# A four-layer graph network on one core: the setup moved into the static plan, six shared PSUM banks, and a plan with other durations

## The chip, the cores and the metric

The kernel runs on one core of one Trainium2 chip. The metric is device time in microseconds (us) of that core, from the first to the last instruction. Five engines work side by side, each through its own queue in program order: TensorE (PE, with its weight loads PEld), VectorE (DVE), ScalarE (ACT), GpSimd (POOL) and SyncE (SP), which here issues nearly all DMA transfers.

## What is computed

64 graphs of 256 nodes with 256 features pass four layers, each with a layer norm before it and a residual after it. Layers 0 and 1 are attention with four heads of 64, layer 2 attention with one head of 256, layer 3 a gated graph network of three rounds.

```python
h = relu(layernorm(x)); x = x + gat0(h, adj)      # 4 heads: softmax over neighbours, elu
h = relu(layernorm(x)); x = x + gat1(h, adj)      # 4 heads, relu + residual, norm per head
h = relu(layernorm(x)); x = x + gat2(h, adj)      # 1 head of 256
h = relu(layernorm(x))
for i in range(3):                                # layer 3
    m = h @ weight[i]
    aggr = A.T @ m                                # A = (adj != 0)
    h = gru_cell(aggr, h, w_ih, w_hh, b_ih, b_hh)
x = x + h
```

`adj` is 0 or 1 (about 1.6% ones), all numbers are fp32.

## The kernel before

The graphs are worked on in 32 pairs. The program is a list of steps, each with its engine, an assumed duration, the steps it needs, and the buffers that it takes and gives back. When the kernel is built, a list scheduler (the plan) goes through these steps, always takes the one that can start first (by rank among those that can start at the same time), and writes its instructions. On the chip each engine runs its instructions in that order and waits on semaphores; the assumed durations act only through the order.

```python
class Plan:
    AFTER = {"PE": 0.25, "DVE": 0.12, "ACT": 0.22, "POOL": 0.2, "SP": 0.1}   # handoff after a step
    ...
    def run(self):
        ...
                t = max(t, clock[s[0]])          # s[0]: the engine
                starts.setdefault(s[0], []).append((t, k))
```

Before the plan stands the setup. It loads the weights, adds columns to them that give the attention scores (multiply by the attention vectors and reduce), and multiplies the GRU's input weights by the layer weights, so that a GRU round needs one product less:

```python
    nc.sync.dma_start(w0e[:, :, :D], w0.rearrange("(c p) f -> p c f", p=P))
    ...                                                   # w1e, w2e, whh, rows of bias, gamma, beta
    with tc.tile_pool(name="setup", bufs=1) as sp, tc.tile_pool(name="setup_ps", bufs=2, space=PSUM) as spp:
        ...                                               # loads of vectors (ACT queue), w3, wih
        for i in range(L):
            for dc in range(DC):
                for g0, g1 in ((0, 512), (512, G)):
                    ps = spp.tile([P, 512], F32, name="ps_wc")
                    for ec in range(DC):
                        nc.tensor.matmul(ps[:, : g1 - g0], lhsT=w3[:, i, ec, dc * P : (dc + 1) * P],
                                         rhs=wih[:, ec, g0:g1], start=(ec == 0), stop=(ec == DC - 1))
                    nc.scalar.copy(wc[:, i, dc, g0:g1], ps[:, : g1 - g0])
```

PSUM is shared out by purpose: `w` (two tiles of two banks: projection and head sums), `t` (one bank, all transposes of the attention part), `g` (three banks, the GRU).

```python
    TILES = {
        "w": tiles("w", 2, [2, S], pool=psum), "t": tiles("t", 1, [S], pool=psum), "g": tiles("g", 3, [S], pool=psum),
        "xt": tiles("xt", 4, [C, D]), "at": tiles("at", 2, [C, N], I32), ...
        "ht3": tiles("ht3", 3, [DC, S]), "hn": tiles("hn", 3, [C, D]), ..., "d": tiles("d", 2, [S]), ...
```

One attention layer of one graph: project, copy the scores out (`scores`, VectorE), transpose them, send them through DRAM so that each partition gets the whole row (`a_b`), then per head exponential (ACT), mask (DVE) and sum (TensorE, 65 columns, the last one gives the denominator):

```python
        k = add("PE", 1.8, emit_project, [g.done], take=[pw, g.wh], give=[g.ht], due=due)
        g.scored = sc = add("DVE", 0.15, emit_scores, [k], due=due)
        wh = add("ACT", 0.57, emit_wh, [k, sc], give=[pw], due=due)
        k = add("PE", 0.12, emit_turn, [sc], take=[turn, er, g.dj], due=due)
        k = add("ACT", 0.45, emit_er, [k], give=[turn], due=due)
        k = add("SP", 0.1, emit_out, [k], give=[er], due=due, lag=2.0)
        load_ = add("SP", 0.1, emit_in, [k], take=[a_b], due=due, lag=3.0)
        k = None
        for h in range(heads):
            x_ = add("ACT", 0.94, lambda h=h: emit_exp(h), [load_, s.has_cap], take=[q[h]], ...)
            x_ = add("DVE", 0.84, lambda h=h: emit_q(h), [x_], ...)
            k = add("PE", 1.8 if heads == 1 else 1.0, lambda h=h: emit_sum(h), [x_, wh, k],
                    take=[] if h else [g.po], give=[q[h]], due=due)
        g.done = add("DVE", 0.17, emit_rs, [k], take=[g.rs], due=due)
```

The layer norm before each layer has its inverse root on GpSimd (`add("POOL", 1.0, emit_root, ...)`) between two VectorE steps. Of the GRU, only this matters here: its difference step writes a buffer `d`, and a pair's GRU is due three periods of 112 us after its attention, so that GRU matmuls of older pairs fill TensorE while younger pairs are in attention.

Of the kernel before, what the change touches and what calls it, by code (L numbers as in the profile page):

```python
# [32 lines left out]
class Plan:  # L33
# [7 lines left out]
    AFTER = {"PE": 0.25, "DVE": 0.12, "ACT": 0.22, "POOL": 0.2, "SP": 0.1}  # L41
# [11 lines left out]
    def run(self):  # L53
# [16 lines left out]
        while ready:  # L70
            best = None
            starts = {}
            for k, t in ready.items():
                s = steps[k]
                for b in s[4]:
                    t = max(t, min(self.free[b.tag])[0]) if self.free[b.tag] else None
                    if t is None:
                        break
                if t is None:
                    continue  # L80
                t = max(t, clock[s[0]])
                starts.setdefault(s[0], []).append((t, k))
# [32 lines left out]
def fast_path(ctx, tc, x, adj, w0, a0_src, a0_dst, w1, a1_src, a1_dst, bias1, gamma1, beta1,  # L115
# [8 lines left out]
    nc = tc.nc  # L124
# [22 lines left out]
    whh = consts.tile([P, DC, G], F32, name="whh")  # L147
    bg = consts.tile([P, 8], F32, name="bg")
# [6 lines left out]

    nc.sync.dma_start(w0e[:, :, :D], w0.rearrange("(c p) f -> p c f", p=P))
    for dc in range(DC):
        nc.sync.dma_start(
            w1e[:, dc, :D].rearrange("p (h e) -> p h e", h=H),
            w1[:, dc * P : (dc + 1) * P, :].rearrange("h p e -> p h e"),  # L160
        )
    nc.sync.dma_start(w2e[:, :, :D], w2t.rearrange("(c p) f -> p c f", p=P))
    nc.sync.dma_start(whh, whh_t.rearrange("(c p) g -> p c g", p=P))
    nc.sync.dma_start(bias_b, _rows(bias1, D))
    nc.sync.dma_start(gamma_b, _rows(gamma1, D))
    nc.sync.dma_start(beta_b, _rows(beta1, D))

    with tc.tile_pool(name="setup", bufs=1) as sp, tc.tile_pool(
        name="setup_ps", bufs=2, space=bass.MemoryType.PSUM
    ) as spp:  # L170
        ab = sp.tile([P, 3, 2, D], F32, name="ab")
        for s, (s0, s1) in enumerate(((a0_src, a1_src), (a0_dst, a1_dst))):
            nc.scalar.dma_start(ab[:, 0, s, :], _rows(s0, D))
            first = bass.AP(tensor=s1.tensor, offset=s1.offset, ap=[[0, P], [T * E, H], [1, E]])
            nc.scalar.dma_start(ab[:, 1, s, :].rearrange("p (h e) -> p h e", h=H), first)
        nc.scalar.dma_start(ab[:, 2].rearrange("p s f -> p (s f)"), _rows(a2, 2 * D))
        w3 = sp.tile([P, L, DC, D], F32, name="w3")
        wih = sp.tile([P, DC, G], F32, name="wih")
        for i in range(L):
            nc.sync.dma_start(w3[:, i], w3t[i].rearrange("(c p) d -> p c d", p=P))  # L180
        nc.sync.dma_start(wih, wih_t.rearrange("(c p) g -> p c g", p=P))
        bi = sp.tile([P, 6], F32, name="bi")
        bh = sp.tile([P, 6], F32, name="bh")
        nc.scalar.dma_start(bi, bih)
        nc.scalar.dma_start(bh, bhh)

        for k, (we, heads) in enumerate(((w0e, H), (w1e, H), (w2e, 1))):
            for dc in range(DC):
                for s in range(2):
                    tmp = sp.tile([P, D], F32, name="tmp", bufs=2)  # L190
                    nc.vector.tensor_mul(tmp, we[:, dc, :D], ab[:, k, s, :])
                    nc.vector.tensor_reduce(
                        we[:, dc, D + s * heads : D + (s + 1) * heads],
                        tmp.rearrange("p (h e) -> p h e", h=heads), AX.X, OP.add,
                    )


        for i in range(L):
            for dc in range(DC):
                for g0, g1 in ((0, 512), (512, G)):  # L200
                    ps = spp.tile([P, 512], F32, name="ps_wc")
                    for ec in range(DC):
                        nc.tensor.matmul(
                            ps[:, : g1 - g0],
                            lhsT=w3[:, i, ec, dc * P : (dc + 1) * P],
                            rhs=wih[:, ec, g0:g1],
                            start=(ec == 0),
                            stop=(ec == DC - 1),
                        )
                    nc.scalar.copy(wc[:, i, dc, g0:g1], ps[:, : g1 - g0])  # L210


        nc.vector.tensor_add(bg[:, 0:4], bi[:, 0:4], bh[:, 0:4])
        nc.vector.tensor_copy(bg[:, 4:6], bh[:, 4:6])
        nc.vector.tensor_scalar_mul(bg[:, 0:6], bg[:, 0:6], 0.5)
        nc.vector.tensor_copy(bg[:, 6:8], bi[:, 4:6])
# [13 lines left out]
    def tiles(tag, count, shape, dtype=F32, pool=bufs):  # L230
# [3 lines left out]
        "w": tiles("w", 2, [2, S], pool=psum),  # L234
        "t": tiles("t", 1, [S], pool=psum),
        "g": tiles("g", 3, [S], pool=psum),
        "xt": tiles("xt", 4, [C, D]),
        "at": tiles("at", 2, [C, N], I32),
# [12 lines left out]
        "ht3": tiles("ht3", 3, [DC, S]),  # L251
        "hn": tiles("hn", 3, [C, D]),
# [4 lines left out]
        "d": tiles("d", 2, [S]),  # L257
# [18 lines left out]

    PERIOD = 112.0
# [5 lines left out]
    def load(p, needs):  # L283
# [10 lines left out]
        s.has_x = add("SP", 0.1, emit_x, needs, take=[s.xt, s.scores], due=s.due, lag=5.0)  # L294
        s.has_a = add("SP", 0.1, emit_a, needs, take=[s.at], due=s.due, lag=5.0)
        return s

    def prepare(s):
# [42 lines left out]
        for b, ps in enumerate((Buf("t"), Buf("t"))):  # L341
            k = add(
                "PE", 0.46, lambda b=b, ps=ps: emit_turn(b, ps), [first, *caps, k],
# [8 lines left out]
    def norm(s, b, needs, sink):  # L352
# [3 lines left out]
        mv, rs, xn, ps = Buf("mv"), Buf("rstd"), Buf("xn"), Buf("t")  # L356
# [36 lines left out]
        k = add("POOL", 1.0, emit_root, [k], take=[rs], due=due)  # L393
        k = add("DVE", 0.82, emit_xn, [k], take=[xn], give=[rs, mv], due=due)
        t = add("PE", 0.46, emit_turn, [k], take=[ps] if sink else [ps, g.ht], give=[] if sink else [xn], due=due)
# [5 lines left out]
    def attend(s, b, g, layer, we, heads, alpha, score0):  # L401
# [4 lines left out]
        pw, turn, er, a_b = Buf("w"), Buf("t"), Buf("er"), Buf("a_b")  # L406
        g.wh = Buf("wh1" if heads == 1 else "wh4")
        g.po, g.dj, g.rs = Buf("w"), Buf("dj"), Buf("rs")
# [5 lines left out]
        def sums_():  # L414
            return g.po.t[:, :, : heads * (e + 1)].rearrange("p c (h e) -> p c h e", h=heads)
# [53 lines left out]
        def emit_sum(h):  # L469
            for ic in range(2):  # L470
                for jc in range(2):
                    nc.tensor.matmul(  # L472
                        g.po.t[:, ic, h * (e + 1) : (h + 1) * (e + 1)],
                        lhsT=q[h].t[:, jc, ic * P : (ic + 1) * P], rhs=g.wh.t[:, jc, h, :],
                        start=(jc == 0), stop=(jc == 1),
                    )

        def emit_rs():
            nc.vector.reciprocal(g.rs.t[:, :, :heads], sums_()[:, :, :, e])

        k = add("PE", 1.8, emit_project, [g.done], take=[pw, g.wh], give=[g.ht], due=due)
# [4 lines left out]
        k = add("SP", 0.1, emit_out, [k], give=[er], due=due, lag=2.0)  # L486
# [162 lines left out]
    def gru_layer(s, i, ht, hn, has_ht, has_hn):  # L649
# [32 lines left out]
        for dc in range(DC):  # L682
# [6 lines left out]
            )  # L689
            has_ag = has_ag + [k]  # L690

        users, has_new = [], []

        def column(j):
            nh, ri, ni, zi = Buf("g"), Buf("g"), Buf("g"), Buf("g")
# [642 lines left out]
```

## Time and profile before

| | |
|---|---|
| time, median of 3 runs | 3726.41 us (3721.69 to 3729.0) |
| profiled span | 3726.5 us, mean granted TensorE clock 0.982 |
| TensorE busy | 3567.1 us, 14577 matmul instructions |
| gate matmuls (128x512) | 4608, 603 and 596 ns each |
| head sums (128x65) | 4096, 278 ns each, paced 0.112 us apart |
| first transpose of a pair | 48.55 us after the start |
| first GRU aggregation | 186.11 us after the start |

Matmuls overlap in the pipeline, so their mean durations are longer than the pace at which they follow each other. Line numbers (L436) are those of the kernel printed above; an entry such as "PE t L436 <- DVE scores L428: 52.1, 16, 3.8" says who waited for whom, how long in all, how often, and the longest. In a timeline line the first two numbers are start and duration in us, and the bracket at its end tells how long the engine had been idle and who released it.

### The profile page before, as it was taken

How to read it: one execution, taken by the hardware profiler on the slowest of the kernel's cores; microseconds unless marked ns; L12 is line 12 of the kernel's file. 1: busy time of each engine (PE TensorE's matmuls, PEld its weight loads, DVE VectorE, ACT ScalarE, POOL GpSimd, SP SyncE). 2: the span in 40 equal slices, each digit the busy share in tenths (PEclk: the TensorE clock that was granted, in tenths of full speed). 3: DMA queues.
4: the chain of work that ended last, by engine and by line, in shares of the span. 5: the costliest groups of instructions: out<-in, count | busy, mean ns of one | idle time of the engine just before them, and what ended most of it. 6: DMA issues, size and time to landing. Idle time of an engine off the chain costs nothing.

```text
span 3726.5 us, 41332 instructions
## 1 busy us (share of the span) xinstructions
PE 3567.1 (96%) x14577; PEld 2258.2 (61%) x14577; DVE 2245.9 (60%) x5282; ACT 1594.5 (43%) x3277; POOL 1011.6 (27%) x1040
## 2 busy tenths in 40 slices
PE   5799999999999999999999999999999999999998
PEld 4565566666565666566666665666666665666654
DVE  4656665665566666565665566666566665665622
ACT  3343444444444444444444444444444444444422
POOL 1322322232222322322232222322223332222211
PEclk8799999999999999999999999999999999999999
DMA  3100101111100011101101111011001111010000
GB/s 115 43 29 29 43 21 43 38 31 52 32 32 32 29 49 32 32 32 43 38 29 45 30 41 33 26 52 32 32 32 43 35 31 43 21 45 30 21 6 12
DMA packets 86023, 133.49 MB, mean 36 GB/s; under 512 B 8368, under 2 KB 68784, under 8 KB 85808
## 3 DMA queue, kind: packets, MB, share of 16 engines
q1 hardware_dynamic: 84032, 129.98, 10.8%
q8 instruction: 117, 1.92, 0.2%
q10 hardware_dynamic: 1776, 0.79, 0.1%
q14 instruction: 98, 0.80, 0.1%
HBM read 113.38 MB, written 17.37 MB: 35 GB/s over the span
## 4 chain that ended last, share of the span: by engine, by line
PE 85%; DVE 7%; POOL 4%; DMA 1%; issue 1%; ACT 1%; SPq 0%; DVEq 0%; ACTq 0%; POOLq 0%
PE g L675 48%; PE w L472 15%; PE g L660 9%; PE w L422 8%; PE t L380 2%; PE g L762 2%; POOL rstd L367 2%; DVE xn L371 1%; PE t L323 1%; DVE xt L530 1%; POOL xm L521 1%; POOL xm L553 1%; DVE st L362 1%; POOL rstd L366 1%; PE t L436 1%
## 5 line engine op out<-in xcount | busy, mean ns | idle before, releaser
L675 PE MATMUL g<-ht,whh 128*128 128x512 f32 x2304 | 1106.8, 603 | 4.5 <-ACT n L699 4.4
L675 PE MATMUL g<-ag,wc 128*128 128x512 f32 x2304 | 1080.3, 596 | 0.0
L675 PEld LDWEIGHTS g<-ag,wc 128*128 128x128 f32 x2304 | 433.5, 192 | 508.5 <-issue 499.6
L716 POOL TENSOR_TENSOR d<-ht,n 128x512 f32<-128x512 f32 x192 | 284.4, 1481 | 1504.5 <-ACT n L713 1504.4
L472 PEld LDWEIGHTS w<-wh,q 128*128 128x128 f32 x4608 | 593.8, 196 | 87.8 <-issue 49.3
L675 PEld LDWEIGHTS g<-ht,whh 128*128 128x128 f32 x2304 | 416.1, 192 | 378.3 <-issue 359.1
L472 PE MATMUL w<-wh,q 128*128 128x65 f32 (+1 forms) x4608 | 619.5, 289 | 17.0 <-DVE q L463 14.1
L463 DVE SCALAR_TENSOR_TENSOR q<-q,dj,cap_t 128x256 f32<-128x256 f32 x1152 | 522.4, 512 | 101.5 <-ACT q L456 97.7
L456 ACT ACTIVATE q<-a_b,scores 128x256 f32<-128x256 f32 x1152 | 499.1, 498 | 136.8 <-DMA a_b<-dr 84.2
L719 DVE SCALAR_TENSOR_TENSOR d<-z,d 128x512 f32<-128x512 f32 x192 | 148.1, 772 | 379.6 <-ACT z L704 358.7
L660 PE MATMUL g<-am,hn 128*128 128x256 f32 x1536 | 363.4, 381 | 0.3 <-ACT z L704 0.3
L660 PEld LDWEIGHTS g<-am,hn 128*128 128x128 f32 x1536 | 286.0, 191 | 74.1 <-issue 34.2
L371 DVE TENSOR_SCALAR xn<-xt,mv,rstd 128x256 f32<-128x256 f32 x512 | 209.9, 431 | 162.2 <-POOL rstd L367 158.3
L704 ACT ACTIVATE r<-g,bg 128x512 f32<-128x512 f32 x192 | 131.6, 686 | 386.7 <-PE g L675 386.7
L707 DVE SCALAR_TENSOR_TENSOR n<-r,n 128x512 f32<-128x512 f32 x192 | 131.8, 686 | 265.2 <-ACT r L704 239.2
L713 ACT ACTIVATE n<-n,bg 128x512 f32<-128x512 f32 x192 | 137.8, 718 | 247.8 <-DVE n L710 247.6
L704 ACT ACTIVATE z<-g,bg 128x512 f32<-128x512 f32 x192 | 131.3, 684 | 258.0 <-PE g L675 253.6
L387 ACT ACTIVATE ht<-t 128x512 f32<-128x512 f32 x256 | 152.0, 594 | 188.7 <-PE t L380 170.3
L699 ACT ACTIVATE n<-g,bg 128x512 f32<-128x512 f32 x192 | 131.9, 687 | 233.6 <-PE g L675 230.4
L380 PEld LDWEIGHTS t<-ident,xn 128*128 128x128 f32 x1024 | 125.8, 145 | 143.2 <-issue 60.3
L362 DVE BATCH_NORM_STATS2 st<-xt 128x6 f32<-128x256 f32 x512 | 192.9, 410 | 26.4 <-DMA xt<-in_x_dram 25.9
L380 PE MATMUL t<-ident,xn 128*128 128x128 f32 x1024 | 170.8, 282 | 30.0 <-DVE xn L371 11.0
(86 smaller groups left out, 3536.2 us busy)
## 6 DMA issues: line engine op xcount, KB each, us to landing
a_b<-dr SPq DMA_DIRECT2D x128, 512.0 KB
xt<-in_x_dram SPq DMA_DIRECT2D x32, 512.0 KB
at<-in_adj_dram SPq DMA_DIRECT2D x32, 512.0 KB
out_dram<-hn SPq DMA_DIRECT2D x32, 512.0 KB
a_b<-dr SPq DMA_DIRECT2D x64, 128.0 KB
dr<-er SPq DMA_DIRECT2D x128, 4.0 KB
dr<-er SPq DMA_DIRECT2D x64, 1.0 KB
whh<-in_L_gnn_w_hh_dram SPq DMA_DIRECT2D x1, 768.0 KB
```

Source lines behind the costliest of these rows:

```text
L362: nc.vector.bn_stats(st[ic].t, s.xt.t[:, 2 * b + ic, :])
L371: nc.vector.tensor_scalar(xn.t[:, ic, :], s.xt.t[:, 2 * b + ic, :], mv.t[:, ic, 0:1], rs.t[:, ic : ic + 1], op0=OP.subtract, op1=OP.mult,)
L380: nc.tensor.transpose(ps.t[:, dc * N + ic * P : dc * N + (ic + 1) * P], xn.t[:, ic, dc * P : (dc + 1) * P], ident,)
L387: nc.scalar.activation(out_, ps.t.rearrange("p (d i) -> p d i", d=DC), AF.Relu)
L422: nc.tensor.matmul(pw.t[:, ic, :m], lhsT=g.ht.t[:, dc, ic * P : (ic + 1) * P], rhs=we[:, dc, :m], start=(dc == 0), stop=(dc == DC - 1),)
L456: nc.scalar.activation(q[h].t[:, jc, :], a_b.t[:, h, :], AF.Exp, scale=1.0 - alpha, bias=scores()[:, heads + h, jc : jc + 1],)
L463: nc.vector.scalar_tensor_tensor(q[h].t[:, jc, :], q[h].t[:, jc, :], g.dj.t[:, h, jc : jc + 1], s.cap_t.t[:, b, jc, :], op0=OP.max, op1=OP ...
L472: nc.tensor.matmul(g.po.t[:, ic, h * (e + 1) : (h + 1) * (e + 1)], lhsT=q[h].t[:, jc, ic * P : (ic + 1) * P], rhs=g.wh.t[:, jc, h, :], sta ...
L660: nc.tensor.matmul(ps_ag[dc].t[:, b * N : (b + 1) * N], lhsT=hn.t[:, 2 * b + sc, dc * P : (dc + 1) * P], rhs=s.am.t[:, 2 * b + sc, :], sta ...
L675: nc.tensor.matmul(ps.t, lhsT=w[:, dc, g * P : (g + 1) * P], rhs=u.t[:, dc, :], start=(k == 0), stop=(k == n - 1),)
L704: nc.scalar.activation(out_.t, ps.t, AF.Tanh, bias=bg[:, k : k + 1], scale=0.5)
L716: nc.gpsimd.tensor_tensor(d.t, ht.t[:, j, :], n.t, op=OP.subtract)
```

## The change

Five things are changed, all in the fast path.

1. **Setup inside the plan.** The weight loads, the score columns and the combined gate weights become steps of the plan. The first pair's x, the weights of layer 0 and the first pair's adjacency are issued first; the rest follows. The temporaries live in buffers that the pairs use later (`hn`, `ag`, `ht3`, `xm`, `o`). All loads go through SyncE.
2. **PSUM.** One pair of banks (`w`) for projections, and six single banks (`b`) for everything else.
3. **Sums by two heads.** The four heads' sums no longer stand in two banks together but two heads in one bank, and are summed, inverted and divided two heads at a time.
4. **Buffers.** One adjacency buffer instead of two, four `ht3` and `hn` instead of three, no `d`: the difference is written to the new state's own place. A pair's GRU waits for the last result of the GRU two before it, no longer for its store.
5. **The plan.** Durations from measurement, shorter handoffs, and a margin of 0.5 us between a TensorE step's inputs and its planned start.

What it is for: TensorE should start on the first pair earlier, wait less for a PSUM bank, and meet its inputs more often ready. Cut to its core:

```diff
-    AFTER = {"PE": 0.25, "DVE": 0.12, "ACT": 0.22, "POOL": 0.2, "SP": 0.1}
+    AFTER = {"PE": 0.22, "DVE": 0.05, "ACT": 0.09, "POOL": 0.09, "SP": 0.05}
+    BEFORE = {"PE": 0.5, "DVE": 0.0, "ACT": 0.0, "POOL": 0.0, "SP": 0.0}
...
-                t = max(t, clock[s[0]])
+                t = max(t + self.BEFORE[s[0]], clock[s[0]])
...
-    nc.sync.dma_start(w0e[:, :, :D], w0.rearrange("(c p) f -> p c f", p=P))
-    ...                                   # the whole setup
...
-        "w": tiles("w", 2, [2, S], pool=psum),
-        "t": tiles("t", 1, [S], pool=psum),
-        "g": tiles("g", 3, [S], pool=psum),
+        "w": tiles("w", 1, [2, S], pool=psum),
+        "b": tiles("b", 6, [S], pool=psum),
-        "at": tiles("at", 2, [C, N], I32),
+        "at": tiles("at", 1, [C, N], I32),
-        "ht3": tiles("ht3", 3, [DC, S]),
-        "hn": tiles("hn", 3, [C, D]),
+        "ht3": tiles("ht3", 4, [DC, S]),
+        "hn": tiles("hn", 4, [C, D]),
-        "d": tiles("d", 2, [S]),
...
+    def fetch(kb, emit, take=()):
+        nonlocal turn, landed
+        turn, landed = turn + 1, landed + kb / 170.0
+        return add("SP", 0.35, emit, take=take, due=1e5 * (turn - 100), lag=landed)
...
+        s0 = load(0, [])
+        w = [fetch(256, emit_w0)]
+        a = [fetch(256, lambda: emit_ab(0), [ab[0]])]
+        s0.has_a = s0.start()
+        s1 = load(1, [])
+        s1.has_a = s1.start()
+        w.append(fetch(256, emit_w1))
+        ...                                # ab, rows, wih, w3, w2, whh, bi
+                    m = add("PE", (g1 - g0) / 300.0, lambda ...: emit_wc(*a), [in_, in3[i]], take=[ps], due=90)
+                    c = add("ACT", 0.2 + (g1 - g0) / 1400.0, ...: emit_copy(*a), [m, *copies[-1:]], ..., due=90)
...
-        k = add("POOL", 1.0, emit_root, [k], take=[rs], due=due)
+        k = add("POOL", 1.1, emit_root, [k], take=[rs], due=due)
...
-        k = add("SP", 0.1, emit_out, [k], give=[er], due=due, lag=2.0)
-        load_ = add("SP", 0.1, emit_in, [k], take=[a_b], due=due, lag=3.0)
+        k = add("SP", 0.35, emit_out, [k], give=[er], due=due, lag=1.5)
+        load_ = add("SP", 0.35, emit_in, [k], take=[a_b], due=due, lag=3.5 if heads == H else 2.5)
...
-                "ACT", 0.94, lambda h=h: emit_exp(h), [load_, s.has_cap], take=[q[h]],
+                "ACT", 1.0, lambda h=h: emit_exp(h), [load_, s.has_cap], take=[q[h]],
-                "DVE", 0.84, lambda h=h: emit_q(h), [x_], give=[g.dj] if end else [],
+                "DVE", 0.96, lambda h=h: emit_q(h), [x_], give=[g.dj] if end else [], due=due
...
+        for k in range(2):
+            need = made if heads == 1 else made[2 * k : 2 * k + 2]
+            give = (q if k else []) if heads == 1 else q[2 * k : 2 * k + 2]
             x_ = add(
-                "PE", 1.8 if heads == 1 else 1.0, lambda h=h: emit_sum(h), [x_, wh, k], take=[] if h else [g.po], ...
+                "PE", 0.87 if heads == 1 else 1.77, lambda k=k: emit_sum(k),
+                [*need, wh, *g.done[-1:]], take=[g.po[k]] + ([] if k else [g.rs]), give=give, due=due,
+            )
+            g.done.append(add("DVE", 0.17, lambda k=k: emit_rs(k), [x_], due=due))
...
-                nc.gpsimd.tensor_tensor(d.t, ht.t[:, j, :], n.t, op=OP.subtract)
+                nc.gpsimd.tensor_tensor(h_new.t[:, j, :], ht.t[:, j, :], n.t, op=OP.subtract)
...
-        return add("SP", 0.1, emit_store, has_hn, give=[hn, ht, s.xt], due=due, lag=3.0)
+        add("SP", 0.35, emit_store, has_hn, give=[hn, s.xt], due=due, lag=3.0)
+        return has_hn[-1]
```

## Prediction

> **What bounds the kernel now.** I read the head of the page first. It names TensorE, and it also shows why that is not the whole answer:
>
> ```profile
> PE 3567.1 (96%) x14577; PEld 2258.2 (61%) x14577; DVE 2245.9 (60%) x5282; ACT 1594.5 (43%) x3277; POOL 1011.6 (27%) x1040
> ```
>
> No other engine is above 61%, so the end is set by TensorE's work plus whatever keeps TensorE from working at full rate. "Busy" does not say how much of the second there is, because an instruction at half clock is as busy as one at full clock. So I worked the pure work out from start times. In stretches of the timeline where nothing waits, one fp32 matmul instruction follows the last at a fixed pace: 0.430 us for 512 columns (four start at 1198.78, the next four at 1200.50), 0.216 for 256 to 264 columns, 0.112 for the 65-column sums (31 from 1211.68), 0.109 for a 128-column transpose. With the counts of the groups (each matmul of the source is two instructions), one pair of graphs needs: gates 144 x 0.430 = 61.9; aggregation 48 x 0.216 = 10.4; projections 48 x 0.22 = 10.6; head sums 128 x 0.112 = 14.3; layer-2 sums 16 x 0.217 = 3.5; transposes 70 x 0.109 = 7.6. That is 108.3 us a pair, 3466 for 32 pairs, and 15.5 for the combined gate weights of the setup (24 x 0.43 + 24 x 0.216): **3481 us of work**. The remaining 245 us are what a change of order, buffers and setup can touch.
>
> Next I looked where those 245 us lie, in the table of stretches (columns: span, busy us and count of PE, weight loads, DVE, ACT, POOL, then granted clock, DMA share, GB/s):
>
> ```profile
> 0.00:22.00 22.00, 0.14 (x1) 0.14 (x1) 8.69 (x28) 1.28 (x1) 0.76 (x8) 1.00 0.64 197
> 22.00:40.00 18.00, 17.80 (x48) 9.19 (x48) 0.00 (x0) 5.54 (x12) 0.14 (x4) 1.00 0.00 0
> 40.00:60.00 20.00, 9.12 (x30) 6.47 (x30) 11.89 (x42) 4.67 (x12) 9.32 (x20) 0.66 0.59 184
> 100.00:120.00 20.00, 16.49 (x76) 15.41 (x76) 16.77 (x39) 8.75 (x20) 4.83 (x6) 0.60 0.10 32
> 140.00:160.00 20.00, 19.88 (x84) 18.51 (x84) 10.59 (x29) 7.05 (x16) 0.00 (x0) 0.53 0.04 18
> 160.00:180.00 20.00, 9.40 (x35) 6.33 (x33) 15.87 (x46) 7.02 (x16) 10.63 (x12) 0.83 0.05 15
> 455.00:3154.00 2699.00, 2635.71 (x10898) 1668.89 (x10899) 1680.70 (x3939) 1188.95 (x2449) 763.14 (x770) 0.99 0.11 36
> 3600.00:3700.00 100.00, 97.66 (x280) 49.52 (x279) 25.20 (x38) 27.47 (x42) 10.11 (x8) 1.00 0.02 6
> 3700.00:3727.00 27.00, 17.95 (x48) 8.10 (x46) 6.72 (x10) 4.50 (x7) 2.53 (x2) 0.91 0.07 23
> ```
>
> Four pieces can be read off. **Setup:** TensorE does nothing for 22 us (weights load), then computes the combined weights while nothing of a pair is loaded (0 GB/s): the inputs are issued only at 39.83, and the first transpose starts at 48.55. Take off 15.5 of work: 33 us. **Ramp, 48.55 to 400:** the ten stretches of the table, of which four stand here, leave 46 us of TensorE idle, and the busy time times the missing clock is another 30: some 80 us. **Tail:** 9 idle in the last stretch and 2 before it: 11. **Steady state:** the rest, 120. The timeline shows most of it as one gap that comes back every second pair:
>
> ```profile
> 1122.32 3.73 PE L422 MATMUL w<-w1e,ht 128*128 128x264 f32 x16
> 1129.82 0.38 PE L436 MATMUL t<-ident,scores 128*8 128x128 f32 x1 [3.78 <-DVE scores L428]
> 1129.99 3.62 PE L675 MATMUL g<-ht,whh 128*128 128x512 f32 x4
> ```
>
> The reader is to see a wait of 3.8 us for the scores' copy, and after it four matmuls in 3.6 us instead of 1.72: the clock is at half. The gap begins at 451.15 and then 12 times more up to 3149.64, so a pair takes 2698.5 / 24 = 112.4 us against 108.3 of work. One gap costs 3.9 of idle and some 2.3 of slow matmuls (about five at 0.86): 6.2, and 13 of them 81. In the chain of waits, TensorE's own list says the same:
>
> ```profile
> PE t L436 <- DVE scores L428: 52.1, 16, 3.8
> PE ps_wc L203 <- DMA wih<-in_L_gnn_w_ih_dram: 21.9, 1, 21.9
> ```
>
> The gap is no shortage of VectorE: from 1118 to 1130 VectorE waits five times on GpSimd's root (2.87 us the longest), and the copy stands behind those in its queue. The order was fixed by a plan that thought VectorE would be there some 4 us earlier. It is an error of the plan.
>
> **What the Trainium skill says.** "TensorE: Matmul & The Clock Gate", Part 1 (the HAM clock gate): after an idle window of about 3.4 us the array falls to half clock and needs a busy window of the same length to come back. The trace agrees: a 3.9 us gap, then clock 0.50 in the stretch 1130 to 1134, where a gap under 1 us (1184.2) brings none. "Perfetto Trace Analysis", Identifying the Most-Contended Engine: matmul busy share is a poor measure of how close one is. It agrees here (140 to 160: busy 19.88 of 20, clock 0.53). "PSUM — Partial Sum Buffer", The four PSUM rules: one matmul output lies in one bank of 512 fp32. Four heads by two row blocks by 65 columns are 520, so the sums took two banks; two heads are 260 and fit in one. "DMA: Bandwidth & Descriptors", Queues, rings and completion order: descriptors of one queue are consumed in ring order. That matters for the new start; the trace of before shows no pair load behind a long queue of others.
>
> **The change part by part.**
> *Setup in the plan.* The first x load is issued first. Before, it took from 39.83 to 43.9, and the first transpose came 4.65 later. Issued at about 0.75, that gives a first transpose near 9.7 (estimate). The idle 33 becomes 10: **-23**. The 15.5 us of weight matmuls move into the ramp, where TensorE is idle 46 us. They come along without lengthening it much, and they keep the clock up.
> *What the loads cost.* 4.3 MB of weights plus 2 MB of two pairs now share one queue. Before, the setup moved 197 GB/s. At that rate the first projection's weights and vectors (1 MB with x) are there at about 2 + 1024/197 = 7 us, but the queue drains only near 30 us, and the first score round trip (ready near 20) has to pass behind it. I charge 5 to 8 us for that.
> *Banks.* Before: two pairs of banks for projection and sums, one bank for all transposes, three for gates. In the ramp the transposes wait for that one bank (ACT ht before the next transpose, or the cap copy before it, 0.8 to 1.1 us, four times between 48 and 63). Six shared banks remove that. The projection alone keeps a bank pair, for 1.78 + 0.15 + 0.57 and handoffs, some 3.2 us, six times a pair: 19 of 108 us.
> *Ramp in sum.* 80, less up to 15 for the absorbed setup, less 5 to 10 for banks, plus 5 to 8 for the queue: **65**. VectorE sets a limit: it needs 2246/32 = 70 us a pair, about 49 of it attention, against 33 of attention on TensorE, so before the first GRU TensorE can't be more than two thirds used.
> *Sums by two heads.* The same matmuls, so no TensorE time. VectorE does 256 divisions of half size (planned 0.4 each, before 128 x 0.68) and twice the reciprocals: 15 + 28 = 43 us more in all, 60% to about 61%. Off the path.
> *Plan.* Durations of the trace (root 1.1 instead of 1.0, exponentials 1.0 instead of 0.94, masks 0.96 instead of 0.84), shorter handoffs, and a TensorE step is placed 0.5 us after its inputs. If this removes the 13 gaps, the steady loss falls from 120 to some 35 (1.2 a pair); I keep 1.4 a pair for 28 pairs: **39**.
> *Tail* unchanged: the last GRU runs the same steps: 11.
> Sum: 3481 + 10 + 65 + 39 + 11 = **3606**.
>
> **Rivals.**
> (a) *The plan is wrong elsewhere.* The order is static, so every step the plan places too early stops TensorE; the old gap was one in 224 us and another may take its place. For it: the new plan has other buffers, so a wholly other order. Against it: durations now match the groups, and the margin covers half a microsecond. With one gap of 6 us per pair the steady loss is 170 and the time 3737; with the old rate, 3606 + 80 = 3686.
> (b) *The start gains little.* The queue holds the round trips and weight matmuls push in front of the first pair. Then the ramp stays at 90 or more: 3630.
> (c) *A shared resource becomes the wait:* the one bank pair of projections or the single adjacency buffer. Before, that load already waits for the mask 198 us in all in the DMA queue without holding anyone. I give this 20 to 40 us at worst: 3640.
>
> **Range and chances.** Certain are only the 23 us of the start and that the work stays. The steady part is the large one, 0 to 100 us; the ramp is +-20. So 3605, and 3558 to 3678 for 8 in 10. 2% faster means under 3652: I need about 74 of the expected 120, which fails if the gaps largely stay or come back elsewhere. Faster 0.79, same 0.17, slower 0.04.
>
> **What would show it.** First transpose near 10 us and weight matmuls spread between 20 and 60. No gap over 3 us after 450, pair period near 109.7, clock 1.00 there. Ramp: fewer stretches under 0.8 of clock. VectorE near 61%. I am wrong if a regular gap over 3 us stands in the steady state, if the first GRU aggregation comes later than about 150 us (186 before), or if the steady period is over 112.

## The result, and the profile after

The kernel after takes **3762.49 us** (median of 4 runs, 3761.74 to 3763.3), the kernel before 3727.7 beside it: a ratio of 1.0096, 95% interval 1.0079 to 1.0114. The change makes the kernel slower by 1%; 3605 was predicted, with a range of 3558 to 3678.

One statement of the chapter on the kernel before has to be taken back first, because everything else hangs on it: "On the chip each engine runs its instructions in that order." It doesn't. The plan writes the instructions in its order, but the framework that builds the program then sorts each engine's instructions once more (the second sorting, from here on). In the built program of the kernel after, 2719 of VectorE's 3821 steps stand in another place than in the plan. Most of the experiments below switch that second sorting off, on all engines or on some.

The head of the page of the kernel after (engine, busy us, share, instructions) shows that the amount of work is what it was, and VectorE's share is near the 61% expected:

```profile
PE 3569.5 (95%) x14577; PEld 2258.3 (60%) x14577; DVE 2263.0 (60%) x5602; ACT 1575.0 (42%) x3277; POOL 1000.3 (27%) x1040
```

The table of stretches of the kernel after (columns as in the prediction: span, busy us and count of PE, weight loads, DVE, ACT, POOL, then clock, DMA share, GB/s):

```profile
0.00:22.00 22.00, 10.21 (x40) 7.63 (x41) 13.94 (x43) 6.67 (x14) 7.89 (x24) 1.00 0.71 239
...
455.00:3154.00 2699.00, 2592.24 (x10663) 1641.41 (x10663) 1653.31 (x4088) 1144.58 (x2383) 738.98 (x749) 0.99 0.11 35
```

The start is better: TensorE has 40 instructions in the first 22 us instead of 1, at 11.16 comes the first transpose (48.55 before), and the first GRU aggregation stands at 130.4 (186.1 before). The steady part is worse: 10663 matmul instructions in the same 2699 us in which the kernel before had 10898.

To put numbers on it I took, for every matmul instruction, the time from its start to the start of the next and subtracted the median of that time for its form (the pace of the prediction). What is left over is loss by waiting and by the slow clock, and it can be added up by stretch. It ends with TensorE's last instruction, some 7 us before the end of the program:

| loss of TensorE, us | to 450 | 450 to 3400 | from 3400 | sum |
|---|---|---|---|---|
| before | 121 | 112 | 8 | 241 |
| after | 82 | 170 | 24 | 276 |
| difference | -39 | +58 | +16 | +35 |

The sum of the differences is the measured loss (3762 - 3728 = 35). So the start brought its 39 us, and the rest lost 74.

The two largest entries in TensorE's own list of waits of the kernel after (total us, times, longest) are both waits for VectorE; no other is above 10.2 us:

```profile
PE b L532 <- DVE scores L524: 84.0, 39, 3.5
PE b L472 <- DVE xn L463: 63.5, 49, 11.2
```

It is the old gap again, and now there is a second one some 40 us behind it, so that most stretches of two pairs have both. TensorE's timeline of the kernel after at one of them (start, duration, instruction; the bracket is the idle time before and who ended it):

```profile
2141.38 1.02 PE L796 MATMUL b<-ht,whh 128*128 128x512 f32 x2
2145.94 0.27 PE L532 MATMUL b<-ident,scores 128*8 128x128 f32 x1 [3.54 <-DVE scores L524]
...
2146.48 2.83 PE L796 MATMUL b<-ht,whh 128*128 128x512 f32 x4
```

After 3.5 us of idling four gate matmuls take 2.83 us instead of 1.88. VectorE and then GpSimd in the same window:

```profile
2141.72 0.16 DVE L455 BATCH_NORM_AGGREGATE mv<-st 128x2 f32<-128x6 f32 x1
2145.00 0.41 DVE L463 TENSOR_SCALAR xn<-xt,mv,rstd 128x256 f32<-128x256 f32 x1 [3.12 <-POOL rstd L459]
...
2145.71 0.17 DVE L524 COPY scores<-w 128x16 f32<-128x16 f32 x1
```

```profile
2139.27 1.54 POOL L482 TENSOR_SCALAR hn<-xn 128x512 f32<-128x512 f32 x1
2140.89 1.50 POOL L636 TENSOR_SCALAR xm<-xt 128x512 f32<-128x512 f32 x1
2142.36 1.49 POOL L482 TENSOR_SCALAR hn<-xn 128x512 f32<-128x512 f32 x1
2143.93 0.22 POOL L458 TENSOR_SCALAR rstd<-mv 128x2 f32<-128x2 f32 x1
```

The copy of the scores (0.17 us) needs nothing but its projection. It stands behind a normalisation (`xn`) that waits 3.12 us for its root, and in GpSimd's queue the root stands behind three row steps, each 1.5 us long. In the plan's own list (its assumed clock, not that of the chip) the copy stands ahead of what overtook it:

```
VectorE in the plan:  2086.51 copy of the scores | 2086.66 copy of hn | 2088.05 statistics | 2089.20 statistics | 2090.44 xn
```

In the program that runs, both statistics and the normalisation come first. So there were two suspects: GpSimd's order (long rows ahead of the root) and VectorE's (the copy behind the normalisation), both made by the second sorting; and against them the plan itself and the new structure.

### The profile page after: what moved, and what is told of

Read it like the earlier page. It is cut to its first block, busy times and chain, and to the rows that moved or that the text cites. A ratio compares the mean times of both kernels' runs of the same rounds, so it can differ in the third digit from the quotient of the medians.

```text
span 3760.0 us, 41566 instructions
## 1 busy us (share of the span) xinstructions
PE 3569.5 (95%) x14577; PEld 2258.3 (60%) x14577; DVE 2263.0 (60%) x5602; ACT 1575.0 (42%) x3277; POOL 1000.3 (27%) x1040
## 4 chain that ended last, share of the span: by engine, by line
PE 72%; DVE 14%; POOL 10%; issue 2%; ACT 1%; DMA 1%; SPq 0%; POOLq 0%; DVEq 0%; ACTq 0%
PE b L796 39%; PE b L569 14%; PE w L518 7%; PE b L781 6%; POOL var L699 3%; PE b L472 3%; POOL rstd L459 2%; DVE xn L463 2%; PE b L885 2%; DVE st L454 1%; DVE ht L843 1%; POOL xm L636 1%; POOL rstd L458 1%; POOL hn L482 1%; DVE o L705 1%
## 5 line engine op out<-in xcount | busy, mean ns | idle before, releaser
L796 PE MATMUL b<-ht,whh 128*128 128x512 f32 x2304 | 1114.1, 604 | 0.8 <-ACT n L820 0.8
L796 PE MATMUL b<-ag,wc 128*128 128x512 f32 x2304 | 1074.1, 593 | 0.0
L796 PEld LDWEIGHTS b<-ag,wc 128*128 128x128 f32 x2304 | 431.5, 191 | 501.9 <-issue 492.9
L569 PEld LDWEIGHTS b<-wh,q 128*128 128x128 f32 x4608 | 587.2, 193 | 105.9 <-issue 67.5
L837 POOL TENSOR_TENSOR ht<-ht,n 128x512 f32<-128x512 f32 x192 | 292.1, 1522 | 1277.3 <-ACT n L834 1196.7
L569 PE MATMUL b<-wh,q 128*128 128x65 f32 (+1 forms) x4608 | 619.2, 287 | 11.7 <-DVE q L559 10.2
L796 PEld LDWEIGHTS b<-ht,whh 128*128 128x128 f32 x2304 | 413.6, 193 | 341.3 <-issue 324.8
L781 PE MATMUL b<-am,hn 128*128 128x256 f32 x1536 | 367.3, 384 | 0.5 <-POOL hn L482 0.5
L781 PEld LDWEIGHTS b<-am,hn 128*128 128x128 f32 x1536 | 290.1, 193 | 63.0 <-issue 24.7
L472 PE MATMUL b<-ident,xn 128*128 128x128 f32 x1024 | 171.9, 288 | 66.1 <-DVE xn L463 63.5
```

Source lines behind the costliest of these rows:

```text
L472: nc.tensor.transpose(ps.t[:, dc * N + ic * P : dc * N + (ic + 1) * P], xn.t[:, ic, dc * P : (dc + 1) * P], ident,)
L569: nc.tensor.matmul(sums_(k) if heads == 1 else sums_(k)[:, ic, h % 2], lhsT=q[h].t[:, jc, ic * P : (ic + 1) * P], rhs=g.wh.t[:, jc, h, :], ...
L781: nc.tensor.matmul(ps_ag[dc].t[:, b * N : (b + 1) * N], lhsT=hn.t[:, 2 * b + sc, dc * P : (dc + 1) * P], rhs=s.am.t[:, 2 * b + sc, :], sta ...
L796: nc.tensor.matmul(ps.t, lhsT=w[:, dc, g * P : (g + 1) * P], rhs=u.t[:, dc, :], start=(k == 0), stop=(k == n - 1),)
L837: nc.gpsimd.tensor_tensor(h_new.t[:, j, :], ht.t[:, j, :], n.t, op=OP.subtract)
```

## Experiments

Each was timed against the kernel before, in the same session. There the kernel before took 3717 to 3721 us, 6 to 10 less than the 3728 beside the kernel after. Differences from the kernel after's 3762 are uncertain by that much.

**The order of the plan kept, on all engines.** The edit is the same for both kernels:

```diff
-    plan.run()
+    with tc.manual_schedule(engines={PE, DVE, Activation, Pool, SP}):   # issue in the order written
+        plan.run()
```

The kernel after (e1):

> The kernel after, with the order of the plan kept on every engine (the framework that builds the program sorts each engine's instructions once more by a timing of its own; here it is told to leave them as the plan wrote them). The plan itself ends at 3646. Theory 1 (the second sorting spoils the plan: GpSimd's long row steps are put ahead of the short roots): 3650 to 3700, and the 3.7 us gap of every second pair (TensorE waiting for the scores' copy) is gone. Theory 2 (the new plan's durations and short handoffs leave no slack, whoever sorts): 3760 or more, gaps of 1 to 4 us all over. Theory 3 (the shared banks, the sums by two heads or the fewer buffers are the cause): about 3760, with waits on PSUM tiles or on the adjacency buffer in place of the waits for the scores.

Measured: **3619.39 us**, ratio 0.9729 (0.9713 to 0.9746). Loss 86 + 34 + 12 = 132 us in the three stretches of the table. TensorE's wait for the scores, 84.0 us before, is now:

```profile
PE b L532 <- DVE scores L524: 8.1, 16, 3.1
```

The regular gap is gone: after 450 us TensorE has no gap over 2.7 us. Theory 1 holds, and the gain is larger than its range. Some 140 us lay in the second sorting, and theories 2 and 3 fall for the plan and the structure as they stand together.

The kernel before (e2):

> The kernel before, with the order of its plan kept in the same way. Its plan ends at 3776 without the setup, some 3816 with it. Theory 1: the second sorting had also spoiled this one, but its plan is poorer: 3690 to 3760, and its own 3.8 us gap every second pair gone. Theory 2: its plan had durations that were too short for GpSimd and the exponentials: 3760 to 3830. Theory 3 says nothing of it: within 1% of 3727.

Measured: 3714.01 us, ratio 0.9983 (0.9973 to 0.9993). TensorE's list of waits of this run:

```profile
PE g L660 <- ACT en L575: 31.4, 13, 2.4
...
PE t L436 <- DVE scores L428: 2.8, 3, 1.4
```

The wait for the scores, 52.1 us before, is down to 2.8. So the old gap too had been made by the second sorting. But another wait stands in the same rhythm, 13 times 2.4 us for ScalarE, and this one is the old plan's own; the loss between 450 and 3400 is 95 instead of 112. Theory 1 holds, with little gain.

**Structure and plan exchanged, second sorting left on (e3, e4).** The kernel after with the old figures of the plan (old handoffs, no margin, root 1.0, exponential 0.94, mask 0.84, and so on), and the kernel before with the new ones:

```diff
-    AFTER = {"PE": 0.22, "DVE": 0.05, "ACT": 0.09, "POOL": 0.09, "SP": 0.05}
-    BEFORE = {"PE": 0.5, ...}
+    AFTER = {"PE": 0.25, "DVE": 0.12, "ACT": 0.22, "POOL": 0.2, "SP": 0.1}
+    BEFORE = {"PE": 0.0, ...}
```

> The kernel after (setup in the plan, six single banks, sums by two heads, buffers) with the old plan: the old handoffs, no margin ahead of TensorE's steps, the old durations. Theory 1: another plan gives another order, which the second sorting changes as well; 3690 to 3760, with no certain side. Theory 2: the loss of the steady part goes away and the 41 us of the start stay: 3680 to 3700. Theory 3: stays at 3750 to 3775.

Measured: 3854.0 us, ratio 1.0357 (1.0339 to 1.0374).

> The kernel before (own setup, old banks, sums of four heads) with the new plan: new durations, short handoffs, 0.5 us of margin. Its plan ends at 3838 without the setup. Theory 1: 3730 to 3800, as the second sorting has it. Theory 2: slower by what the change lost in its steady part, about 76 us: 3790 to 3810. Theory 3: 3715 to 3735, as before.

Measured: 3852.8 us, ratio 1.0352 (1.0335 to 1.0369).

Both are outside every range that I had written, and above both whole kernels. Theory 2 named a side for the first and theory 3 for the second, and both sides were wrong. As long as the second sorting is on, these exchanges don't tell what a part is worth.

**Structure and plan exchanged, with the plan's order kept (e5, e6).**

> The structure of the change (setup in the plan, six banks, sums by two heads, buffers) with the old handoffs and durations and no margin, the order of the plan kept. Its plan ends at 3732. With the order kept, the kernel before took 3714 and the kernel after 3619. Theory A (the structure makes the 95 us): 3620 to 3660. Theory B (the durations and the margin make them): 3690 to 3720, since only the start's 41 us come off at most. Theory C (the two need each other): 3660 to 3690.

Measured: 3679.18 us, ratio 0.9887 (0.9871 to 0.9904).

> The structure of before with the new durations, handoffs and margin, the order of the plan kept. Its plan ends at 3838 without the setup, 62 later than with the old figures. Theory A (structure): 3700 to 3730, like before with its order kept. Theory B (durations and margin): 3640 to 3670. Theory C (they need each other; with one bank for all transposes a margin of 0.5 us on TensorE costs at each of them): 3730 or more.

Measured: 3805.57 us, ratio 1.0237 (1.022 to 1.0255). TensorE waits for the GRU's new state on VectorE:

```profile
PE g L763 <- DVE ht L723: 57.4, 33, 7.9
```

With the old figures and the order kept that wait was 26.7 us.

With the order kept the four corners are:

| us | old figures of the plan | new figures |
|---|---|---|
| old structure | 3714 | 3806 |
| new structure | 3679 | 3619 |

This is theory C. The structure alone brings 35 us, the new figures alone cost 92, and both together bring 95. The first run lies in the range of theory C (3660 to 3690) and the second is above 3730. Why the old structure suffers from the new figures was not shown; the waits for one transpose bank that theory C names are not the largest in the list.

**The margin alone (e7).** As in the kernel after with the order kept, but `BEFORE = {"PE": 0.0, ...}`:

> The kernel after with the order kept and the margin of 0.5 us ahead of TensorE's steps taken out, all else as it is. Its plan ends at 3684 instead of 3646. If the margin is what keeps TensorE from waiting: 3650 to 3690, with waits of 0.5 to 2 us through the steady part. If it does nothing: 3610 to 3630.

Measured: 3701.37 us, ratio 0.9947 (0.9927 to 0.9967), a little over the range: with this structure and these durations the half microsecond in the plan is worth 82 us. Without it the plan puts the transposes of the new GRU state where VectorE hasn't delivered yet:

```profile
PE b L885 <- DVE ht L847: 64.9, 14, 7.1
```

With the margin this wait is 12.3 us in 7 waits. Without it the new durations and short handoffs are even 22 us slower than the old figures (3679).

**The six single banks (e11).** Order kept on all engines, and

```diff
-        "w": tiles("w", 1, [2, S], pool=psum),
-        "b": tiles("b", 6, [S], pool=psum),
+        "w": tiles("w", 2, [2, S], pool=psum),
+        "b": tiles("b", 4, [S], pool=psum),
```

> The kernel after with the order kept on every engine (3619 so far), but with two pairs of banks for the projection and four single banks, instead of one pair and six. Its plan ends at 3718 instead of 3646. If the six single banks are what the structure brings: 3670 to 3720. If it is the setup in the plan and the sums by two heads: 3615 to 3640.

Measured: 3778.01 us, ratio 1.0154 (1.0134 to 1.0174), worse than the range. The head sums now wait for a bank that ScalarE has to empty:

```profile
PE b L569 <- ACT er L538: 23.6, 13, 3.6
```

The loss between 450 and 3400 is 157 instead of 34, 123 of the 159 us. More than half of that is not waiting: by the trace's clock record TensorE is busy at half clock for 148 us of this stretch (10 with six banks), which costs some 69 us. The slow stretches, mostly 10 us long, start at such a wait for a bank, as here, where 48 sums of 0.112 us take 8.36:

```profile
902.17 8.36 PE L569 MATMUL b<-wh,q 128*128 128x65 f32 x48 [1.96 <-ACT er L538]
```

The wait for `xn` grows too, from 22.1 to 53.0. So with the new figures the six banks are not a detail of the structure but what carries it. How much the sums by two heads bring by themselves was not tried.

**Which engine's order (e8, e9, e10).** The kernel after, with the plan's order kept on VectorE and GpSimd, on GpSimd alone, and on VectorE alone:

```diff
-    plan.run()
+    with tc.manual_schedule(engines={DVE, Pool}):       # then {Pool}, then {DVE}
+        plan.run()
```

> The kernel after with the order of the plan kept on VectorE and GpSimd alone; TensorE, ScalarE and SyncE are sorted again by the framework. If the harm is done on these two engines (long row steps ahead of roots, the scores' copy behind them): 3615 to 3660, the 3.7 us gap gone. If it is TensorE's or ScalarE's own order: 3720 to 3765.

Measured: 3614.34 us, ratio 0.9714 (0.9698 to 0.9731). Nothing is lost by leaving the other three engines to the second sorting.

> The kernel after with the plan's order kept on GpSimd alone. With VectorE and GpSimd kept it took 3614, with none kept 3762. If the harm is what the trace of the kernel after shows (three long row steps of GpSimd ahead of the short root, VectorE waiting for it with the scores' copy behind): 3615 to 3660, the 3.7 us gap gone. If it is VectorE's own order: 3730 to 3765.

Measured: 3758.92 us, ratio 1.01 (1.0084 to 1.0117).

> The kernel after with the plan's order kept on VectorE alone. If GpSimd's order does the harm: 3720 to 3765, VectorE still waiting up to 3 us for the root. If VectorE's does: 3615 to 3660.

Measured: 3636.33 us, ratio 0.9771 (0.9755 to 0.9788).

My reading of the gap was half wrong. GpSimd's order alone brings nothing measurable (ratio 1.01 against 1.0096 for the kernel after), VectorE's some 120 us; GpSimd's brings another 22 once VectorE's is kept. TensorE and then VectorE, in the run with GpSimd's order kept, at the same place of the program:

```profile
2144.89 0.38 PE L532 MATMUL b<-ident,scores 128*8 128x128 f32 x1 [3.06 <-DVE scores L524]
```

```profile
2143.77 0.38 DVE L463 TENSOR_SCALAR xn<-xt,mv,rstd 128x256 f32<-128x256 f32 x1
2144.07 0.68 DVE L847 SCALAR_TENSOR_TENSOR ht<-ht,n 128x512 f32<-128x512 f32 x1
2144.67 0.16 DVE L524 COPY scores<-w 128x16 f32<-128x16 f32 x1
```

Here VectorE is busy nearly all the time, and TensorE still waits 3.06 us. (Part of it is the first half of this normalisation: it starts at 2141.81 and takes 1.35 us instead of 0.38, beside a 1.26 us step of GpSimd that starts at 2141.75. Whether the one slows the other was not tried.) This gap is at the copy of the projection just before the one shown above: a normalisation (its second half is the first line here) and a step of the GRU (L847) have been put ahead of it. In the run with both orders kept, TensorE and then VectorE at both copies:

```profile
2070.29 0.27 PE L532 MATMUL b<-ident,scores 128*8 128x128 f32 x1
...
2074.42 0.27 PE L532 MATMUL b<-ident,scores 128*8 128x128 f32 x1 [0.81 <-DVE scores L524]
...
2074.96 1.88 PE L796 MATMUL b<-ht,whh 128*128 128x512 f32 x4
```

```profile
2069.52 0.17 DVE L524 COPY scores<-w 128x16 f32<-128x16 f32 x1
2069.61 0.68 DVE L847 SCALAR_TENSOR_TENSOR ht<-ht,n 128x512 f32<-128x512 f32 x1
...
2074.20 0.17 DVE L524 COPY scores<-w 128x16 f32<-128x16 f32 x1
...
2074.88 0.41 DVE L454 BATCH_NORM_STATS2 st<-xt 128x6 f32<-128x256 f32 x1
```

The first copy is ahead of L847 now, and TensorE's transpose has no wait at all. The second is ahead of the statistics, its gap is 0.81 us, and the four gate matmuls after it run at full clock (1.88).

**Which of VectorE's steps (e13, e14).** The second sorting stays on; only some orders are held. In the first run the twelve VectorE steps that the plan puts after a copy of the scores stay behind it; in the second the statistics and normalisations stay behind the twelve VectorE steps before them:

```diff
-            emit()
+            with ExitStack() as stack:
+                for ins in held:                         # copies of the last 12 steps, or the last 12 steps
+                    stack.enter_context(self.tc.issue_after(ins))
+                emit()
```

> The kernel after, sorted again by the framework as usual, but with one order held: on VectorE, the twelve steps that the plan puts after a copy of the scores stay behind it. If the misplaced copy is what costs the time (TensorE waits for it in the two largest gaps of every second pair, some 80 us with the slow clock after them): 3670 to 3700. If the loss is spread over VectorE's whole order: 3730 to 3765, and other waits for VectorE come in its place.

Measured: 3654.83 us, ratio 0.9826 (0.9809 to 0.9842).

> The kernel after, sorted again as usual, but with the layer norm's statistics and normalisations held behind the twelve VectorE steps that the plan puts before them (they are what the second sorting pulls ahead most often). If this pulling ahead is the harm: 3620 to 3670, near the 3636 of VectorE's order kept as a whole. If the copy alone matters, or the many other small moves: 3690 to 3765.

Measured: 3719.45 us, ratio 1.0003 (0.9994 to 1.0011).

TensorE's wait for the scores and for `xn`, first with the copies held, then with the statistics held (the edit moves the line numbers):

```profile
PE b L481 <- DVE xn L472: 66.3, 42, 12.8
PE b L541 <- DVE scores L533: 18.3, 15, 2.5
```

```profile
PE b L480 <- DVE xn L471: 101.3, 67, 12.9
...
PE b L540 <- DVE scores L532: 9.7, 16, 2.5
```

Holding the place of the 192 copies, each of 0.17 us or less, brings 108 of the 148 us that both engines' orders bring (100 of 142 by the ratios), more than I had expected (3670 to 3700). Their own wait falls from 84.0 us to 18.3, and the loss between 450 and 3400 from 170 to 75: besides the 66 us of shorter waits, TensorE is busy at half clock for 21 us of this stretch instead of 57, which gives another 18. Holding the statistics also takes the wait for the scores away, to 9.7, but the held normalisations now come late themselves: the wait for `xn` grows from 63.5 to 101.3. It is a shift of the wait, and the time falls by 43 only (35 by the ratios).

**What is left at the start (e12, e15).** In the run with both orders kept TensorE stands 15.2 us inside the first projection, and VectorE 16 us in front of an x:

```profile
26.55 0.43 DVE L454 BATCH_NORM_STATS2 st<-xt 128x6 f32<-128x256 f32 x1 [15.96 <-DMA xt<-in_x_dram]
```

I took it for the second pair's x and gave that a landing at 27 us in the plan (order kept on VectorE and GpSimd in this and the next two runs):

> The kernel after with the order kept on VectorE and GpSimd (3614 so far), and with the second pair's x assumed to land at 27 us instead of 14 in the plan (in the trace it landed at 26.5, and VectorE stood 16 us before its first statistics, with the score columns of layer 0 behind it). If that stall is on the path: TensorE's wait inside the first projection (16 us) goes, 3600 to 3608. If the ramp is limited by VectorE's work anyway: 3612 to 3620.

Measured: 3627.04 us, ratio 0.9749 (0.9733 to 0.9766): 13 us slower than without, and VectorE still stands 18.5 us. It was the third pair's x, which the plan takes to land 5 us after its issue though it stands in the queue behind all the weights:

```diff
-            s.has_x = add("SP", 0.35, emit_x, needs, ..., lag=5.0)
+            s.has_x = add("SP", 0.35, emit_x, needs, ..., lag=24.0 if p < 4 else 5.0)
```

> The kernel after with the order kept on VectorE and GpSimd (3614), and with the x of the third and fourth pair assumed to land 24 us after issue instead of 5 (it was issued at 20.5 behind all weights and landed at 26.5). If VectorE's stand for this x, ahead of the score columns of layer 0, is the 16 us wait of the first projection and lies on the path: that wait under 2 us and 3598 to 3606. If the ramp is bound by VectorE's work anyway: 3610 to 3625.

Measured: 3614.3 us, ratio 0.9722 (0.9706 to 0.9738). The 15 us wait is gone (loss to 25 us: 29 before, 17 now), and the time is the same, because the stretch from 25 to 100 loses 30 instead of 16. Up to 450 it is 82 in both. The stall was hidden behind whatever bounds the ramp; VectorE's work is the suspect, but a run that takes work off it was not made.

**A margin for VectorE too (e16).** The same with `BEFORE = {"PE": 0.5, "DVE": 0.2, ...}`:

> As the run before, with a margin of 0.2 us ahead of VectorE's steps as well as 0.5 ahead of TensorE's; its plan ends at 3629 instead of 3648. If slack in the plan is what keeps TensorE fed: 3580 to 3600. If 0.5 on TensorE is enough and more only shifts steps: 3600 to 3640.

Measured: **3595.76 us** (3588.75 to 3598.64), ratio 0.9667 (0.9651 to 0.9683), the fastest version of all, in its range, 18.5 us under the run before it and 3.3% under the kernel before. Its loss is 79 + 27 + 2 = 108. The steady stretch of the run with both orders kept, and then of this one:

```profile
455.00:3154.00 2699.00, 2677.50 (x11140) 1706.28 (x11139) 1808.97 (x4255) 1197.37 (x2489) 739.64 (x775) 1.00 0.11 36
```

```profile
455.00:3154.00 2699.00, 2687.99 (x11233) 1717.77 (x11231) 1845.48 (x4306) 1213.73 (x2526) 759.51 (x791) 1.00 0.11 37
```

## Why the prediction was wrong, step by step

**What failed** is the step on the gap: "The order was fixed by a plan that thought VectorE would be there some 4 us earlier. It is an error of the plan." From it came "If this removes the 13 gaps, the steady loss falls from 120 to some 35", the largest gain of the sum. The gap was real, with its 3.8 us and its slow clock, but not the plan's: with the plan's order kept, the kernel before has it no more (52.1 to 2.8 us of waiting), and the kernel after has no such gap after 450 us. It was made by the second sorting (in the kernel after, of VectorE's queue: keeping that queue alone took the time to 3636), which the change doesn't touch, so new durations and a margin didn't remove it. Instead of falling from 120 to 39, the steady loss rose (112 to 170 in the table of losses). I had read the order of the source as the order of the program. VectorE's timeline of the kernel before could have told:

```profile
1118.93 0.41 DVE L371 TENSOR_SCALAR xn<-xt,mv,rstd 128x256 f32<-128x256 f32 x1 [2.87 <-POOL rstd L367]
1119.26 0.17 DVE L363 BATCH_NORM_AGGREGATE mv<-st 128x2 f32<-128x6 f32 x1
1119.35 0.38 DVE L371 TENSOR_SCALAR xn<-xt,mv,rstd 128x256 f32<-128x256 f32 x1
```

The two normalisations are one step, written by one call; an instruction of another step between them is something that the plan never writes.

With the order kept on all engines, the prediction's sum can be held against e1 term by term. (The prediction's ramp ends at 400 and its tail begins at 3600; the measured stretches end at 450 and begin at 3400.)

| us | predicted | after | after, order kept (e1) |
|---|---|---|---|
| start and ramp (to 450) | 10 + 65 | 82 | 86 |
| steady | 39 | 170 | 34 |
| tail | 11 | 24 | 12 |
| time | 3605 | 3762 | 3619 |

That 3619 comes so near to 3605 is in part luck. The prediction took the gap for the whole steady gain; with the gap gone, the old plan and structure still lose 95 there (e2). The 34 of e1 need the six banks and the margin as well, to which the prediction gave no steady term of their own.

**Start: right.** Predicted were 38 us less (23 of the idle head, 15 of the ramp), measured 39. First transpose 11.16 (estimate 9.7), weight matmuls from 23.4 to 58.8 (20 to 60), first GRU aggregation 130.4 (under 150). The 5 to 8 us set aside for the shared queue were not measured by themselves.

**Work: right.** The same 14577 instructions at the same paces.

**Sums by two heads: open.** 43 us more of VectorE were worked out. Between the two kernels as built it is 17 (2245.9 to 2263.0), with the order kept on both 58 (2308.0 to 2366.0), other changes included. That it lies off the path was not tried by itself.

**Margin and banks: right in direction, and larger than I said.** I gave no term to the margin by itself; with the order kept it is 82 us (e7). For the banks I set 5 to 10 us in the ramp; with the order kept, four single banks instead of six cost 159 us, 123 of them in the steady part (e11). It is the plan with these banks that fits; in the old structure the new figures cost 92. Durations were not tried by themselves: together with the shorter handoffs, but without the margin, they are 22 us slower than the old figures.

**The rivals.** (a), one gap of 6 us per pair and 3737, is close to what happened: two pairs have gaps of 3.5 and some 3 us, often with slow matmuls behind them, and a pair takes 114.3 us. Its steady loss of 170 is the measured one to the microsecond, by chance. But its reason ("every step the plan places too early stops TensorE") isn't the one shown. (b) fell. (c) isn't what TensorE waits for: the projections wait 9.1 us in all for their bank pair in the kernel after, and to give two single banks for a second pair costs (e11). The load into the single adjacency buffer waits longer in its queue for the mask (364.7 us against 198.2), but no wait of TensorE names it; two such buffers were not tried.

**The markers worked.** "A regular gap over 3 us in the steady state" and "a steady period over 112" were named as signs of being wrong, and both came. On the slow clock, the Trainium skill ("TensorE: Matmul & The Clock Gate", Part 1, the HAM clock gate) says half clock after an idle window of about 3.4 us. The pair shown above fits: 3.54 us of idling and then 2.83 us for four matmuls, 0.81 and then 1.88. But the length of a gap doesn't settle it. The same 3.54 us gap at 1688.51 is followed by four gate matmuls in 1.88, and of the thirteen gaps of 2.4 us in the kernel before with its order kept, six are followed by half clock and seven are not. One of each (from the end of the gap on; the third number from the end is the clock):

```profile
1032.30:1036.30 4.00, 3.96 (x20) 3.49 (x21) 3.83 (x10) 1.51 (x3) 3.18 (x4) 1.00 0.00 0
1255.20:1259.20 4.00, 4.00 (x15) 3.38 (x16) 3.83 (x10) 1.55 (x3) 3.24 (x4) 0.67 0.00 0
```

So half clock can follow gaps well under 3.4 us too, here and in e11; what decides it stays open. And on the queue, "Perfetto Trace Analysis" (Tensor Engine Instruction) says that VectorE's and GpSimd's queues are strict FIFO. The trace agrees: the 0.17 us copy waits behind a 3.12 us wait that has nothing to do with it. That makes the order in the built program decisive.

**What stays open:** by what rule the framework sorts, and so why the old plan lost 7 us by it and the new one some 140; what bounds the ramp; and what the sums by two heads, the single adjacency buffer and the fourth `ht3` do by themselves.

## What to carry to other kernels

If a kernel schedules itself, first make sure that the built program has that order: compare the order in the trace with the order written, or keep it by force, before any figure of the schedule is tuned or blamed. When TensorE waits for a short instruction, look at what stands ahead of it in its own queue; holding 192 copies of 0.17 us in their place was worth over 100 us here. And slack written into the schedule can pay: 0.5 us ahead of TensorE's steps was worth 82 us, 0.2 ahead of VectorE's another 18. It does not pay everywhere: in the old structure the new figures, the 0.5 us among them, cost 92.

## What was not expected of the hardware

A statistics instruction is followed later by an aggregation that reads its result than by one that, mostly, doesn't. In the run with the order kept on VectorE and GpSimd the aggregation starts 0.430 us after the statistics that it reads (median of 512). Where the second sorting puts the two row blocks' instructions side by side in the kernel after, 0.326 us pass (median of some 220 aggregations that follow a statistics instruction, most of them another block's). That is up to 512 x 0.104 = 53 us of the 108 us by which VectorE's busy time rises when its order is kept (2263.0 to 2371.5). So the second sorting does save VectorE some busy time, and costs TensorE more. VectorE's 66% isn't the bound: in the fastest version it is busier still (2387.2 us).
